# A fused four-layer kernel on one core: grid operations one unit earlier, five copies on another engine, a transposition around a matmul, and a rebuilt opening

## The chip, the core and the metric

One NeuronCore of a Trainium2 chip. Its engines run their own instruction queues in order: TensorE (PE; its weight loads are listed as PEld), VectorE (DVE), ScalarE (ACT), GpSimd (POOL) and SyncE (SP, which here issues most transfers). They wait for each other through semaphores only. The metric is device microseconds of one launch. Everything is float32.

## What is computed

Eight images of 512 x 512 pass through four layers. Cut to what matters:

```python
# L0: one step on a grid; A_grid and B_grid are the same for all eight images
df = -(grad(A0*f, 1) + grad(A1*f, 2)) + 0.5 * (grad2(B0*f, 1) + grad2(B1*f, 2) + 2 * cross(B2*f))
x = maximum(f + df * dt, 0)               # one-sided formulas on the four edges
# L1: attention, 16 heads of 32, and a feed-forward of 2048
x = ln(x) * (1 + scale) + shift           # scale, shift = silu(sin_emb(t)) @ W_ada + b_ada
q, k, v = x @ Wq + bq, x @ Wk + bk, x @ Wv + bv
p = softmax(where(mask, -inf, q @ k.T / sqrt(32) + attention_bias))
x = x + (p @ v) @ Wo + bo
x = x + gelu((ln(x) * g2 + beta2) @ W1 + b1) @ W2 + b2
# L2: one expert of eight per image, the same shape, and a layer norm
# L3: x + strength * response, through a basis of rank 32
```

## The kernel before

The program has three stages, one after the other. `grid_stage` does L0 for image 0 and prepares all that the others need. `attention_stage` does the attention of all eight images, and in the shadow of it L0 for images 1 to 7. `mlp_stage` does both feed-forwards and L3. Rows are spread as (p r): row 4p + r lies on partition p. Nearly every instruction is emitted under `keep_in_program_order`, so the order of the code is the order on each engine; nothing is left to a planner.

**The opening** (`fused_kernel` and `grid_stage`). Loads go out on SP in this order: the coefficient arrays B and A, image 0 (f), `W_ada`, then `load_w` with Wq, Wk, Wv and Wo, then the small rows of `load_rows`. Tiny vectors go out on ACT's queue. Eight hardware semaphores are shared by all SP and ACT transfers in turn, so that a transfer is issued only after the one eight places before it has landed. VectorE builds six coefficient planes (ca, cb, cc, ce, cg, and b2 on ACT) and their products with f (e, g, c, ga, gb, q, t); TensorE adds these up over the rows in four PSUM tiles `l0_r` with an identity or a shifted identity (`add`). The planes are written to DRAM from POOL's queue (`coef_q` and so on) for the later images. The first and last row of all images are computed at once on 64 partitions: `edge_in` loads their inputs, `fe` from the images and `ec` from the coefficients, the latter eight times by a broadcast DMA; the result `xe` is put into image 0 by four small DMAs `x<-xe` and into DRAM (`xed`). TensorE then computes the embedding (`pe`), and image 0 is normed (`stats`, `pow` on POOL, four `tensor_scalar`) and turned by TensorE (`x1_in`).

**A unit of attention.** `units` runs over image b, group of four heads c and row class r, 16 to an image; t = 4c + r numbers them. The loop at the end of `attention_stage` works, for unit i, on `softmax` of unit i, on `turned` of unit i-1, on `values` of unit i-2, and ends with `scores` of unit i+1. Between these it interleaves the jobs of `fill`: blocks of q, k, v and o, each of four matmuls of 512 columns, in two halves. `softmax` is an add and row minimum on VectorE from the scores in PSUM, and an exponential on ACT. `turned` transposes the probabilities on TensorE, four 128 x 128 pieces for each of the four heads into a PSUM tile `tr` of which there are two, and copies each tile to `pt`: the first head of a pair (i == 0) on VectorE, the second on ACT. `scores` writes four PSUM tiles s0 to s3, one buffer each, so a score of the next unit waits until VectorE has read that of this one. `divide`, once in four units, turns the reciprocal sums (`rb`) and scales the context.

**The grid of the next image** is done in these units. `GRID` is a table written by hand: 17 places j, each with operations on half an image: q, e, g, c, a, b are products of a coefficient plane with f, w a difference of two q, capitals and signs are adds into the image, hh the ghost columns, x the step in time, s and n the norm. For image n, places 0 to 7 fall in the units t = 8 to 15 of image n-2, and places 8 to 16 in the units t = 0 to 8 of image n-1. A bar splits a place into a part before and one after `divide`. `grid_early` runs places 0 to 7 of image 1 ahead of the loop. `grid_gate` makes POOL wait for the last grid operation of the unit before, after which it adds the mask to the bias tiles (`add_mask`, two operations of 128 x 1024) of the unit after. `x1_in` transposes the next image's x in unit t = 9, in four pieces, of which two share VectorE and two ACT for the eviction.

Of the kernel before, what the change touches and what calls it, by code (L numbers as in the profile page):

```python
# [11 lines left out]
F32 = mybir.dt.float32  # L12
# [3 lines left out]
AF = mybir.ActivationFunctionType  # L16
# [4 lines left out]
NB = 8  # L21
# [18 lines left out]
def fused_kernel(ctx: ExitStack, tc: tile.TileContext, a: dict):  # L40
# [65 lines left out]
    nc.scalar.dma_start(freq, a["c_freq"])  # L106
    bada = ep.tile([P, 2 * KC], F32, name="bada")
    nc.scalar.dma_start(bada, a["b_ada"])
    nc.scalar.dma_start(sigs, a["safety"][None, :].to_broadcast([P, NB]))
    nc.scalar.dma_start(eidx, a["eidx"][None, :])  # L110
    nc.vector.tensor_scalar(bada[:, 0:KC], bada[:, 0:KC], 1.0, None, ALU.add)
# [27 lines left out]
    nc.scalar.activation(sigs, sigs, AF.Sigmoid)  # L139
# [14 lines left out]

    def embed_out(pe):
        tc.keep_in_program_order(
            nc.vector.tensor_tensor(
                ada, pe, bada[:, :, None].to_broadcast([P, 2 * KC, NB]), ALU.add
            )
        )  # L160
# [4 lines left out]
    def load_w():  # L165
        for n in ("Wq", "Wk", "Wv", "Wo"):
            w[n] = w8(wo8, n)
            nc.sync.dma_start(w[n], a[n].rearrange("(k p) m -> p k m", p=P))
# [5 lines left out]
    def load_rows():  # L174
        nc.sync.dma_start(bqk[:, 0, :], a["bq"])
        nc.sync.dma_start(bqk[:, 1, :], a["bk"])
        nc.sync.dma_start(bvc, a["bv"].rearrange("(k p) -> p k", p=P))
        nc.sync.dma_start(bo, a["bo"][None, :].to_broadcast([P, D]))
# [3 lines left out]
        embed_out,  # L182
# [3 lines left out]
    io = ctx.enter_context(tc.tile_pool(name="io", bufs=1))  # L186
    g2 = const.tile([P, 2, KC], F32, name="g2")
    nc.scalar.dma_start(g2[:, 0, :], a["g2"])
    nc.scalar.dma_start(g2[:, 1, :], a["beta2"])
    b1 = const.tile([P, NJ], F32, name="b1")  # L190
    nc.scalar.dma_start(b1, a["b1"])
# [4 lines left out]
        g2, mhalf,  # L196
# [18 lines left out]
def grid_stage(  # L215
    tc, a, const, small, dram, x, mhalf, ident, load_wada, load_w, load_rows, embed,
    embed_out,
# [27 lines left out]
    with ExitStack() as ctx:  # L245
# [22 lines left out]
        pin(nc.gpsimd.memset(ec, 0.0))  # L268
# [7 lines left out]
        with tc.tile_pool(name="raw", bufs=1) as rp:  # L276
            a0, b0, a1, b1 = (
                rp.tile([P, R, D], F32, name=k) for k in ("a0", "b0", "a1", "b1")
            )

            def edge_in(i, k):
                lo, hi = max(0, W * k - 1), min(D, W * k + W + 1)
                u = slice(lo - W * k + 1, hi - W * k + 1)
                p0 = n * i
                pin(nc.gpsimd.dma_start(fe[p0 : p0 + n, :, u], a["edge_f"][:, :, lo:hi]))
                for side in range(2):
                    p1 = p0 + side * NB
                    pin(
                        nc.gpsimd.dma_start(
                            ec[p1 : p1 + NB, :, u],  # L290
                            a["edge_c"][side : side + 1, :, lo:hi].to_broadcast([NB, 12, hi - lo]),
                        )
                    )

            halves = slice(0, 2), slice(2, 4)
            for h in halves:
                rows_in(b1, a["B"][1], h)
                rows_in(a1, a["A"][1], h)
            rows_in(b0, a["B"][0])
            rows_in(a0, a["A"][0])  # L300
            rows_in(f, a["x"][0])
            rows_in(b2, a["B"][2])
            nc.scalar.dma_start(gw, a["c_ghost"].to_broadcast([P, 16]))
            nc.scalar.dma_start(dth, a["dt"][None, :].to_broadcast([P, NB]))
            load_wada()
            load_w()
            load_rows()
            pin(nc.gpsimd.memset(zi, 0.0))
            pin(nc.gpsimd.tensor_copy(zi[:, 0, 1 : P + 1], ident))
            pin(nc.gpsimd.tensor_scalar_mul(zi[:, 1, 1 : P + 1], ident, -1.0))  # L310
            gate = small.tile([P, 1], F32, name="gate_e", tag="gate_e", bufs=1)
            pin(nc.gpsimd.tensor_tensor(gate, f[:, 0, 0:1], f[:, 0, 0:1], ALU.add))
            for i, k in enumerate(blocks):
                edge_in(i, k)

            for h in halves:
                tt(ca[:, h, :], b1[:, h, :], a1[:, h, :], ALU.add)
                tt(cb[:, h, :], b1[:, h, :], a1[:, h, :], ALU.subtract)
            tt(cc, b0, b1, ALU.add)
            pin(nc.scalar.mul(cc, cc, -2.0))  # L320
            tt(ce, a0, b0, ALU.add)
            tt(cg, b0, a0, ALU.subtract)
            pin(nc.scalar.mul(b2, b2, 0.5))


        wp = ctx.enter_context(tc.tile_pool(name="l0", bufs=1))
# [54 lines left out]
        for m, w, o in (  # L381
            ("q", b2, 1), ("e", ce, 1), ("c", cc, 0), ("g", cg, 1), ("a", ca, 0), ("b", cb, 0)
        ):
            coefs[m] = dram.tile([S + 2 * o, D], F32, name=f"coef_{m}")
            pin(
                nc.gpsimd.dma_start(
                    coefs[m][o : o + S, :].rearrange("(p r) j -> p r j", r=R), w
                )
            )
            if m in "qe":  # L390
                pin(nc.gpsimd.dma_start(coefs[m][0:1, :], w[0:1, 0, :]))
            if m in "qg":
                pin(nc.gpsimd.dma_start(coefs[m][S + 1 : S + 2, :], w[P - 1 : P, R - 1, :]))
# [83 lines left out]
        xed = dram.tile([n, D], F32, name="xed")  # L477
        for i, k in enumerate(blocks):
            pin(nc.gpsimd.dma_start(xed[:, W * k : W * k + W], xe[n * i : n * i + n, :]))
        pe = embed(ps)  # L480
        pin(nc.vector.tensor_scalar(dth, dth, 0.5, None, ALU.mult))
        st = small.tile([P, R, 6], F32, name="ln0_st", tag="ln0_st", bufs=1)
        mv = small.tile([P, R, 2], F32, name="ln0_mv", tag="ln0_mv", bufs=1)
        for r in (0, 3, 1, 2):
            stt(x[:, r, :], acc[r], dth[:, 0:1], f[:, r, :], ALU.mult, ALU.add)
            pin(nc.scalar.activation(x[:, r, :], x[:, r, :], AF.Relu))
        for o, u, c in ((0, 3 * n, 0), (n, n, 2 * W)):
            for side, q_ in ((0, nc.sync), (1, nc.scalar)):
                p, r = side * (P - 1), side * (R - 1)
                e0 = o + side * NB  # L490
                pin(
                    q_.dma_start(
                        x[p : p + 1, r, c : c + 2 * W].rearrange("o (b w) -> o b w", w=W),
                        xe[e0 : e0 + u + 1 : u, :],
                    )
                )
# [24 lines left out]
def attention_stage(  # L521
    tc, a, small, xp, xt, x_home, x1d, grid, ident, sc1, shift, io, wo8, w, rows,
    g2, mhalf,
# [11 lines left out]
    with ExitStack() as ctx:  # L535
        wp = ctx.enter_context(tc.tile_pool(name="aw", bufs=1))
        pp = ctx.enter_context(tc.tile_pool(name="ap", bufs=2))
        ps = ctx.enter_context(tc.tile_pool(name="a_ps", bufs=1, space=PSUM))
# [85 lines left out]
        def k_block(b, c, tag="m"):  # L624
            pr = ps.tile([P, S], F32, name=f"pk_{b}_{c}", tag=tag)
            half = block(
                pr, lambda k: w["Wk"][:, k, c * P : (c + 1) * P], lambda k: x1s[b, k]
            )
            yield half(0)
            yield half(1)  # L630
            t = pp.tile([P, S], F32, name=f"kt_{b}_{c}", tag="kt")
            pin(nc.scalar.activation(t, pr, AF.Identity, bias=bqk[:, 1, c : c + 1]))
            ks[b, c] = t

# [100 lines left out]
        def grid_op(n, op):  # L735
# [62 lines left out]
            0: "q0 q1", 1: "e0 |", 2: "w0 c0 hh", 3: "C0", 4: "+0 -0", 5: "g0 |", 6: "G0 a0",  # L798
            7: "A0 b0 B0", 8: "x0 q2", 9: "e1 | w1 c1", 10: "C1 +1", 11: "-1 g1", 12: "G1 s0",
# [84 lines left out]
        def fill(b, t):  # L884
# [17 lines left out]
            elif t in (1, 5, 9):  # L902
                jobs.append(k_block(b, t // 4 + 1))
            elif t in (2, 3, 6, 7):
                if b:
                    jobs.append(o_block(b - 1, (2, 3, 6, 7).index(t)))
            elif n < NB:
                if t == 11:
                    jobs.append(q_block(n, 0))
                elif t == 13:  # L910
                    jobs.append(k_block(n, 0))
                else:
                    jobs.append(v_block(n, (10, 12, 14, 15).index(t)))
            if n < NB:
                if t == 9:
                    jobs.append(x1_in(n, c) for c in range(KC))
# [67 lines left out]
        def turned(b, c, r, u):  # L984

            bt = bias.pop((b, c, r, u))
            for i in range(2):
# [9 lines left out]
                if i == 0:  # L997
# [49 lines left out]
        load_bias(*units[0])  # L1047
        grid_loads(1, -1)
        mask_in(0, 1)
        load_bias(*units[1])  # L1050
        for c in range(KC):
            x1_in(0, c)
        mask_out(0, 0)
# [3 lines left out]
        grid_early(0)  # L1057
# [5 lines left out]
        mask_in(0, 3)  # L1063
        grid_early(2)
# [44 lines left out]
def mlp_stage(tc, a, small, xp, io, wo8, x1d, ident, eidx, sigs, layernorm, rstd_of, phalf, wl3, g2, b1, first):  # L1109
# [19 lines left out]
    with ExitStack() as ctx:  # L1129
        wp = ctx.enter_context(tc.tile_pool(name="fw", bufs=1))  # L1130
        ap = ctx.enter_context(tc.tile_pool(name="fa", bufs=2))
        ps = ctx.enter_context(tc.tile_pool(name="f_ps", bufs=2, space=PSUM))
# [725 lines left out]
```

## Time and profile before

| | us |
|---|---|
| median of 3 runs | 2807.26 |
| lowest and highest run | 2805.81, 2810.29 |
| the profiled execution, its time | 2809.32 |
| its span, first to last instruction | 2807.5 |

The 1.8 us between the profiled execution's time and its span lie outside the instructions. The stages, from the busy time of each engine in stretches of the span:

| stretch, us | what | PE busy | DVE busy | ACT busy | POOL busy | granted PE clock |
|---|---|---|---|---|---|---|
| 0 to 60 | opening | 33.4 | 43.9 | 11.2 | 24.0 | 0.99 |
| 60 to 107 | norm of image 0, first units | 37.2 | 35.3 | 12.3 | 11.8 | 0.83 |
| 107 to 230 | rest of image 0 | 116.4 | 104.2 | 78.0 | 66.5 | 0.96 |
| 230 to 359 | image 1 | 126.5 | 112.9 | 83.9 | 71.2 | 1.00 |
| 1034 to 1145 | image 7, no grid beside it | 101.7 | 64.1 | 59.4 | 41.2 | 0.97 |
| 1145 to 2050 | feed-forward of L1 and on | 905.0 | 569.0 | 170.0 | 528.1 | 1.00 |
| 2050 to 2807 | experts and L3 | 746.7 | 444.2 | 149.7 | 383.0 | 0.99 |

A line of a timeline in what follows gives start, duration, engine, line of the code, operation, output and inputs, and how many instructions were merged. A bracket at its end is the time that the engine stood idle before it, and what released it. TensorE's durations include waits inside a merged group: four scores take 1.14 us when nothing holds them.

### The profile page before, as it was taken

How to read it: one execution, taken by the hardware profiler on the slowest of the kernel's cores; microseconds unless marked ns; L12 is line 12 of the kernel's file. 1: busy time of each engine (PE TensorE's matmuls, PEld its weight loads, DVE VectorE, ACT ScalarE, POOL GpSimd, SP SyncE). 2: the span in 40 equal slices, each digit the busy share in tenths (PEclk: the TensorE clock that was granted, in tenths of full speed). 3: DMA queues.
4: the chain of work that ended last, by engine and by line, in shares of the span. 5: the costliest groups of instructions: out<-in, count | busy, mean ns of one | idle time of the engine just before them, and what ended most of it. 6: DMA issues, size and time to landing. Idle time of an engine off the chain costs nothing.

```text
span 2807.5 us, 39790 instructions
## 1 busy us (share of the span) xinstructions
PE 2729.1 (97%) x14654; PEld 2011.6 (72%) x14654; DVE 1942.0 (69%) x3581; ACT 1002.8 (36%) x2133; POOL 1503.9 (54%) x1081
## 2 busy tenths in 40 slices
PE   5999999999999998999999999999999999999998
PEld 3455555555555554788888888888888888888886
DVE  6888898988888766576666756655466556556554
ACT  1466666666666666212111211211121121121221
POOL 3455555555555654466566655656456545535633
PEclk9999999999999999999999999999999999999998
DMA  9665657566666554542533444253223133143120
GB/s 300 225 204 180 235 172 241 186 223 214 194 233 191 157 160 158 181 121 49 158 124 83 109 143 124 49 169 120 73 97 125 59 137 128 42 154 113 42 75 31
DMA packets 190400, 405.62 MB, mean 144 GB/s; under 512 B 24104, under 2 KB 28784, under 8 KB 183934
## 3 DMA queue, kind: packets, MB, share of 16 engines
q1 hardware_dynamic: 185192, 391.93, 42.2%
q0 software_dynamic: 3680, 11.07, 3.2%
q8 instruction: 117, 1.92, 0.3%
q14 instruction: 77, 0.63, 0.1%
q10 hardware_dynamic: 1334, 0.07, 0.0%
HBM read 367.32 MB, written 31.50 MB: 142 GB/s over the span
## 4 chain that ended last, share of the span: by engine, by line
PE 86%; DVE 9%; ACT 2%; DMA 2%; issue 1%; SPq 0%; DVEq 0%; ACTq 0%; POOL 0%
PE y L1137 28%; PE u L1137 28%; PE tr L546 6%; PE s L543 4%; PE ctx L543 4%; PE o L543 3%; PE pv L543 3%; PE pq L543 3%; PE pk L543 2%; DVE bt L973 2%; DVE x L663 2%; DVE pt L998 1%; DMA Wo<-in_Wo 1%; ACT bt L978 1%; PE po L1137 1%; PE btr L1140 1%
## 5 line engine op out<-in xcount | busy, mean ns | idle before, releaser
L1137 PE MATMUL y<-wo,act 128*128 128x256 f32 x2560 | 578.9, 381 | 0.0
L950 POOL TENSOR_TENSOR bt<-bt,mk 128x1024 f32<-128x1024 f32 x256 | 543.2, 2142 | 64.2 <-DMA bt<-in_bias 61.2
L1137 PEld LDWEIGHTS y<-wo,act 128*128 128x128 f32 x2560 | 479.4, 190 | 82.2 <-issue 20.6
L978 ACT ACTIVATE bt<-bt,mn 128x512 f32<-128x512 f32 x512 | 365.4, 715 | 115.5 <-DVE mn L973 115.4
L546 PEld LDWEIGHTS tr<-ident,bt 128*128 128x128 f32 x2048 | 228.2, 141 | 167.7 <-issue 115.7
L1137 PE MATMUL u<-bt,wi 128*128 128x256 f32 x1440 | 330.5, 379 | 0.0
L973 DVE CUSTOM_DVE_ANT_0 bt<-s,bt 128x512 f32<-128x512 f32 x512 | 330.4, 682 | 0.0
L1143 DVE TENSOR_TENSOR act<-u,u 128x512 f32<-128x512 f32 x256 | 173.3, 686 | 209.9 <-PE u L1137 132.6
L1137 PEld LDWEIGHTS u<-bt,wi 128*128 128x128 f32 x1440 | 273.5, 190 | 37.2
L546 PE MATMUL tr<-ident,bt 128*128 128x128 f32 x2048 | 279.9, 278 | 18.8 <-DVE pt L998 7.7
L998 DVE COPY pt<-tr 128x512 f32<-128x512 f32 x256 | 175.8, 687 | 113.3 <-PE tr L546 113.0
L1137 PE MATMUL u<-tb,ws 128*128 128x256 f32 x1024 | 242.1, 379 | 0.0
L1137 PE MATMUL y<-t,s 128*128 128x256 f32 x1024 | 234.2, 380 | 0.0
L1000 ACT COPY pt<-tr 128x512 f32<-128x512 f32 x256 | 148.1, 579 | 183.1 <-PE tr L546 180.7
L1137 PEld LDWEIGHTS u<-tb,ws 128*128 128x128 f32 x1024 | 194.4, 190 | 26.5
L1146 POOL TENSOR_TENSOR t<-wo,t 128x512 f32<-128x512 f32 x64 | 104.5, 1647 | 200.5 <-PE y L1137 200.5
L1137 PEld LDWEIGHTS y<-t,s 128*128 128x128 f32 x1024 | 191.1, 190 | 24.1
L1457 ACT ACTIVATE act<-act,b 128x512 f32<-128x512 f32 x128 | 82.9, 711 | 292.4 <-DVE act L1143 292.4
L1457 ACT ACTIVATE act<-act,bi 128x512 f32<-128x512 f32 x128 | 83.8, 713 | 282.6 <-DVE act L1143 282.6
L1143 DVE TENSOR_TENSOR x<-y,x 128x512 f32<-128x512 f32 x96 | 64.5, 685 | 159.0 <-PE y L1137 105.1
L543 PE MATMUL s<-kt,qt 32*128 32x512 f32 x1024 | 171.7, 645 | 2.3 <-DVE mn L973 1.4
L1143 DVE TENSOR_TENSOR u<-u,u 128x512 f32<-128x512 f32 x192 | 131.3, 684 | 58.8 <-PE u L1137 58.8
(314 smaller groups left out, 4283.5 us busy)
## 6 DMA issues: line engine op xcount, KB each, us to landing
bt<-in_bias SPq DMA_DIRECT2D x256, 512.0 KB
wo<-in_W SPq DMA_DIRECT2D x32, 1024.0 KB
wi<-in_Wi SPq DMA_DIRECT2D x32, 1024.0 KB
wo<-in_Wo_e SPq DMA_DIRECT2D x32, 1024.0 KB
wi<-in_W SPq DMA_DIRECT2D x28, 1024.0 KB
gq<-coef_q SPq DMA_DIRECT2D x21, 512.0 KB
x1d<-x SPq DMA_DIRECT2D x8, 1024.0 KB
x<-x1d SPq DMA_DIRECT2D x8, 1024.0 KB
```

Source lines behind the costliest of these rows:

```text
L543: pin(nc.tensor.matmul(out, lhsT=lhsT, rhs=rhs, start=start, stop=stop))
L546: pin(nc.tensor.transpose(out, src, ident))
L663: pin(nc.vector.tensor_tensor(out, x, y, op))
L950: nc.gpsimd.tensor_tensor(bt, bt, mask[b, r][:, None, :].to_broadcast([P, 2, S]), ALU.add)
L973: nc.vector.tensor_tensor_reduce(bt[:, i, :], ss[h], bt[:, i, :], -1.0, 3.0e38, ALU.add, ALU.min, mn)
L978: nc.scalar.activation(bt[:, i, :], bt[:, i, :], AF.Exp, bias=mn, scale=-1.0, accum_out=sums[b, c, r][:, h : h + 1],)
L998: pin(nc.vector.tensor_copy(pt[:, :, r % 2, :], tr))
L1000: pin(nc.scalar.copy(pt[:, :, r % 2, :], tr))
L1137: pin(nc.tensor.matmul(out, lhsT=lhsT, rhs=rhs, start=start, stop=stop))
L1143: pin(nc.vector.tensor_tensor(out, x, y, op))
L1146: pin(nc.gpsimd.tensor_tensor(out, x, y, op))
L1457: nc.scalar.activation(acts[g][:, k, :], acts[g][:, k, :], func, bias=bi[:, j : j + 1])
```

## The change

- `GRID`: w0, C0, +0, g0, G0 and A0 come earlier by one place; q0, q1, e0, c0, hh, -0, a0, b0, B0 and the places from 8 on stay. `grid_early(0)` is called ahead of the first q block.
- `turned`: the first copy of a unit's first pair goes to ACT when the unit turned is t = 1, 3, 5, 7 or 15 of an image, so it is issued in the next unit (t = 2, 4, 6, 8 and 0). That is 40 copies in all.
- `k_block` in unit t = 9 takes `turn`: the first two transpositions of the next x stand between the third and the fourth matmul of k, the other two behind the eviction of k.
- The opening: the coefficients' edge rows are loaded once, on 8 partitions (`ec8`), and spread to 64 by four matmuls with a selection matrix (`sel8`) and four ACT copies. Wv and Wo are loaded behind the first bias tiles, the vectors g2, beta2 and b1 later still. The tiny vectors move from ACT's queue to SP's. The edge rows are put into x as soon as rows 0 and 3 are done, on SP and ACT; the DRAM copy `xed` moves from POOL's queue to ACT's.
- Eight pools get `reuse_waits="tile"`: a tile waits for those that held its memory, no longer for all of the closed pool's.

```diff
+    nc.sync.dma_start(sigs, a["safety"][None, :].to_broadcast([P, NB]))
+    nc.scalar.activation(sigs, sigs, AF.Sigmoid)
...
-    def load_w():
-        for n in ("Wq", "Wk", "Wv", "Wo"):
+    def load_w(*names):
+        for n in names:
...
-    io = ctx.enter_context(tc.tile_pool(name="io", bufs=1))
+    io = ctx.enter_context(tc.tile_pool(name="io", bufs=1, reuse_waits="tile"))
...
+            for i, k in enumerate(blocks):
+                c, u = edge_cols(k)
+                pin(nc.gpsimd.dma_start(ec8[2 * i : 2 * i + 2, :, u], a["edge_c"][:, :, c]))
...
+            for i in range(4):
+                pec = ps.tile([N, 3, W + 2], F32, name=f"pec_{i}", tag="pec", bufs=2)
+                mm(
+                    pec, sel8.rearrange("q s b -> q (s b)"), ec8[:, 3 * i : 3 * i + 3, :],
+                    True, True,
+                )
+                pin(nc.scalar.copy(ec[:, 3 * i : 3 * i + 3, :], pec))
...
         for r in (0, 3, 1, 2):
             stt(x[:, r, :], acc[r], dth[:, 0:1], f[:, r, :], ALU.mult, ALU.add)
             pin(nc.scalar.activation(x[:, r, :], x[:, r, :], AF.Relu))
+            if r == 3:
+                edges()
+        xed = dram.tile([n, D], F32, name="xed")
+        for i, k in enumerate(blocks):
+            pin(nc.scalar.dma_start(xed[:, W * k : W * k + W], xe[n * i : n * i + n, :]))
...
+        def k_block(b, c, tag="m", turn=None):
+            pr = ps.tile([P, S], F32, name=f"pk_{b}_{c}", tag=tag)
+            for k in range(KC):
+                mm(
+                    pr, w["Wk"][:, k, c * P : (c + 1) * P], x1s[b, k], k == 0, k == KC - 1
+                )
+                if k == 1 or k == (2 if turn else 3):
+                    yield
+                if turn and k == 2:
+                    turn(0)
+                    turn(1)
             t = pp.tile([P, S], F32, name=f"kt_{b}_{c}", tag="kt")
             pin(nc.scalar.activation(t, pr, AF.Identity, bias=bqk[:, 1, c : c + 1]))
             ks[b, c] = t
+            if turn:
+                turn(2)
+                turn(3)
...
         GRID = {
-            0: "q0 q1", 1: "e0 |", 2: "w0 c0 hh", 3: "C0", 4: "+0 -0", 5: "g0 |", 6: "G0 a0",
-            7: "A0 b0 B0", 8: "x0 q2", 9: "e1 | w1 c1", 10: "C1 +1", 11: "-1 g1", 12: "G1 s0",
+            0: "q0 q1", 1: "e0 | w0", 2: "c0 hh C0", 3: "+0", 4: "-0 g0", 5: "G0 |", 6: "a0 A0",
+            7: "b0 B0", 8: "x0 q2", 9: "e1 | w1 c1", 10: "C1 +1", 11: "-1 g1", 12: "G1 s0",
...
-                if i == 0:
+                if i == 0 and not (u == 0 and 4 * c + r in (1, 3, 5, 7, 15)):
                     pin(nc.vector.tensor_copy(pt[:, :, r % 2, :], tr))
...
         load_bias(*units[0])
+        load_w("Wv")
         grid_loads(1, -1)
         mask_in(0, 1)
         load_bias(*units[1])
+        load_w("Wo")
         for c in range(KC):
             x1_in(0, c)
+        grid_early(0)
...
         drain(q_block(0, 0))
-        grid_early(0)
         grid_early(1)
...
         mask_in(0, 3)
+        load_late()
         grid_early(2)
```

## The prediction

> **What bounds the kernel now.** I read the page's busy times first, then the chain of work that ended last, then TensorE's timeline image by image. The page says that TensorE sets the pace nearly everywhere, and has one weak slice at the start:
>
> ```profile
> PE 2729.1 (97%) x14654; PEld 2011.6 (72%) x14654; DVE 1942.0 (69%) x3581; ACT 1002.8 (36%) x2133; POOL 1503.9 (54%) x1081
> PE   5999999999999998999999999999999999999998
> ```
>
> The first digit is a slice of 70 us at half: the opening is not TensorE's. The feed-forwards (1145 to 2807 us) are full and untouched, so the change can win only in the opening and in small gaps of attention. The chain in order of time (start, duration, what) says what ends last in the opening, and VectorE's timeline shows what it waits for:
>
> ```profile
> 26.67 34.86 DMA Wo<-in_Wo
> 61.56 3.29 DMA x<-xe
> ...
> 70.00 3.42 PE xtr L546 x16
> ...
> 77.56 4.28 DVE gq L663 x2
> ...
> 90.64 3.05 DVE x L663
> ...
> 106.57 0.60 DVE pt L998
> ```
> ```profile
> 64.76 0.69 DVE L499 BATCH_NORM_STATS2 ln_st<-x 128x6 f32<-128x512 f32 x1 [7.64 <-DMA x<-xe]
> ```
>
> Up to 61.5 us the chain is a transfer: the small edge DMA x<-xe could not be issued before Wo, eight transfers ahead of it, had landed; VectorE stands 7.64 us for it. From 77.56 to about 118 us the chain is VectorE without a break. For attention I took image 2; its neighbours repeat it to 0.02 us, with a period of 128.97 us:
>
> ```profile
> 361.40 1.06 PE L546 MATMUL tr<-ident,bt 128*128 128x128 f32 x8 [0.32 <-DVE pt L998]
> 364.12 1.35 PE L543 MATMUL s<-kt,qt 32*128 32x512 f32 x8
> 378.15 0.66 PE L546 MATMUL tr<-ident,bt 128*128 128x128 f32 x4 [0.80 <-DVE pt L998]
> 380.46 1.85 PE L543 MATMUL s<-kt,qt 32*128 32x512 f32 x8
> 389.44 1.14 PE L543 MATMUL s<-kt,qt 32*128 32x512 f32 x8
> 409.53 1.26 PE L546 MATMUL tr<-ident,bt 128*128 128x128 f32 x8 [0.70 <-ACT pt L1000]
> 412.45 1.85 PE L543 MATMUL s<-kt,qt 32*128 32x512 f32 x8
> 437.67 1.34 PE L546 MATMUL xtr<-ident,x 128*128 128x128 f32 x8 [0.47 <-DVE x L588]
> 439.23 0.66 PE L546 MATMUL rb<-ident,rw 128*128 128x128 f32 x4 [0.22 <-DVE x L588]
> ```
>
> The reader is to see that TensorE stalls only in units t = 0, 2, 4, 6, 8 (VectorE late with a copy or with reading the scores: 1.85 or 1.35 us where a free group takes 1.14) and in t = 9 (xtr). Adding brackets and stretch: t0 0.32+0.21, t2 0.80+0.71, t4 0.21, t6 0.70+0.20+0.71, t8 0.16, t9 0.47+0.28+0.22, together 5.0 us an image. Units 10 to 15 have none.
>
> **Copies to ACT.** 40 copies leave VectorE (0.69 us each, 0.60 from start to start) and cost ACT 0.58. ACT is busy 84 of 129 us. What stands behind the copy on ACT is the second copy, and the third transposition waits for that one (in the program the third waits for ACT, the fourth for the first copy). So each unit needs ACT's slack today: from the end of the second copy to the start of the third transposition it is 1.0 us in t0, t4, t8 (0.9), 0.68 in t2, none in t6, where ACT comes late from two norm operations (1.51 us).
> - t2: VectorE begins the scores at 377.4, not 378.0, and reads the last at 380.5; the third transposition keeps its 376.7 and the fourth no longer waits. The scores end some 0.25 late: 1.51 less 0.25, gain 1.26.
> - t0, t4, t8: stalls of 0.53, 0.21, 0.16 are all under 0.6 and go.
> - t6: the second copy ends at 409.9, not 409.4, so the third transposition starts 0.42 later than today; the stretch of the scores (0.71) and of the transposition (0.20) goes: gain about 0.45.
>
> Sum 2.6 an image, for the six images (1 to 6) that have grid work there: 15.7 us. Image 7 has none of these stalls: 0. Image 0 is paced by VectorE and stalls more (2.37 us before xb in t6, 1.10 and 0.63 behind), but its copy of x from xb holds the same buffers: 1.5 us, between 0 and 6, since its clock also fell (granted 0.60 in 152 to 160 us).
>
> A rule speaks against this. The Trainium skill's "ScalarE: Activation LUTs", Rules for kernel authors, gives such cheap operations to VectorE, up to about three times faster in bf16. At three times 0.69 a copy would hold ACT 2.1 us, overrun every slack above by over 1 us and cost 40 us. The rows for this copy, f32 out of PSUM, say 579 ns on ACT and 687 on VectorE; I take the rows.
>
> **The turn around k.** Between the second and third xtr there will be one k matmul (two passes, 0.86 us). VectorE evicts the first xtr behind its scores at 436.1 to 436.9, and k ends at 437.2: 0.47 and 0.28 go. The third piece's eviction then holds rb by some 0.3 as today by 0.22. k's own eviction comes 1 us later, not needed before t = 11. Gain 0.5, in seven images: 3.5 us; bounds 0 and 0.97.
>
> **The grid moves.** No instruction is added. w0 (1.2 us) comes behind divide in t = 9, so VectorE's first copy of t = 10 is at 441.9, not 441.6; its transposition buffer is needed at 443.6, so it is hidden by the v matmuls (1.72 us); without that cover it would cost 0.9 an image. C0 (1.35) ends t = 10 at 449.1, when the next transposition ends. t = 15 loses A0 (1.2), which helps t0. POOL's gate now follows C0 or w0; the masks it releases (4.2 us) are read a unit (8 us) later. Cost 0.
>
> **The opening.** (a) ACT's first table load starts behind seven DMA issues, one of them waiting, at 7.67; with two issues left it can start at about 2, and Sin, which VectorE's chain awaits, at 9.1, not 10.5: 1.4. (b) SP issues its first six transfers without a wait (today the third waits until 5.81), so VectorE's waits for A and B (1.01, 0.38, 0.23) go: 1.6. (c) So e and all of TensorE's row sums (26.58 to 54.5, no gap) come 3.0 earlier. (d) The edge loads: 0.39 MB in small packets, while DMA moved only 195 to 232 GB/s from 28 to 40 us at a full share against about 400 before and after, i.e. 12 x 190 kB = 2.3 MB or 5.7 us lost. Instead 49 kB at the start, four matmuls and four copies. None is in the trace: nearest, 0.86 us cold a pass for 512 columns and 0.58 a copy; both engines are empty there (PE until 26.58, ACT 6.4 us before cc), so 0, at worst 2.3 if the first loads land after 23. VectorE's wait for ec (1.63) goes too, hidden under the sums. (e) Wv and Wo leave the queue: 2.1 MB at 0.41 MB/us is 5.1 us. With (d), transfers no longer end last. What is late next is TensorE: sums done at 51.4, embedding at 63.4 - 3.0 = 60.4. Rows 0 and 3 are ready at 51.5; x<-xe takes 3.3 (row above), under the coefficient writes perhaps 6; ACT holds the other two relus behind two issues (0.5 each), in the shade of that landing. From landing to xtr today 5.2 us (statistics, pow, norm). So xtr starts between 60.5 and 63; I take 61.3: 8.7 earlier. The four xed issues on ACT (2.0 us on POOL) have 6 us free there.
>
> Here a second rule: "TensorE: Matmul & The Clock Gate", Part 1, halves the clock after an idle window of about 3.4 us. The gap before xtr (6.64) closes, so by the rule xtr and the first q would run at full clock, 1.3 to 2 us more. But the granted clock here was 0.85 in 58 to 60 and 0.50 in 60 to 62, while the embedding's 8-column matmuls still ran; closing the gap does not keep it up. I take 0.
>
> (f) q0 and q1 now precede qt: VectorE stood 3.25 us for pq at 76.89, and fills that, if gq has landed. The loads of f, q and bias can go out at about 55, not 65, as they wait for single tiles; ahead of x<-coef_e stands Wv, ahead of gg Wo, 2.5 us each, against 10 us gained. C0 moves ahead of the first softmax and out of POOL's way: POOL's two mask adds stretched it to 3.12 from 1.35. This ends with the first softmax near 79.3 (90.6 today), v then holds TensorE until 91.5, and the first copy of pt comes at 94.8 instead of 106.5: 11.7 less, bounds 5 and 15.
>
> **The handover.** The first matmul of the feed-forward no longer waits for VectorE's last o (0.88): VectorE's differences follow at once, so I take 0.6. Other pool waits are nothing's last.
>
> **Sum.** 15.7 + 1.5 + 3.5 + 11.7 + 0.6 = 33.0. Against the profiled execution 2809.3 - 33 = 2776; this execution lay 2.1 above the median shown, so 2774.
>
> **Rivals.**
> - *The opening gives little* (0.20): x<-xe waits under 6.3 MB of coefficient writes and q0 waits for gq. For: small DMAs under load took 4.5 to 6.5 us early on (g2 issued at 7.30 held SP until 13.80). Against: those writes should end near 53. Opening 5: 2781.
> - *The gaps of attention stay* (0.11): ACT's second copy is late in every unit, and what VectorE gains is lost. For: t6 already waits for ACT. Against: slack in four of five. Only opening, turn and handover, 15.8: 2791.
> - *Slower* (0.03): the same mechanism past the balance. In each of 40 places the second copy holds the third transposition by a whole copy, 0.58: 23.2 lost, 15.8 gained, 2815. It decides from 0.40 us a place.
> - *The change does not act* (0.02): a wait that remains, such as one for a shared semaphore, keeps x<-xe where it is and the loads with it, and attention wins as little: 2807.
>
> **Numbers.** The forecast (opening and gaps) has 0.64: 2763 to 2784 by its bounds (image 0 to 6, turn to 6.8, opening to 15, copies up to the full stalls; below, opening 8 and t6 nothing). The range that takes in the rivals but the last two is 2763 to 2790. About 0.2%, 5.6 us, is what a measurement can tell from no change: faster 0.95, within 0.02, slower 0.03.
>
> **What will show it.** Right: xtr at 60 to 63; no 7.64 us wait for x<-xe; the first pt near 95; an image in 125.9 us (128.97 now), score groups of 1.14 in t0, t4, t6, t8; in t6 a longer wait for ACT's pt, in t9 none of 0.47. Wrong: transpositions in t0, t2, t4 held by ACT; VectorE idle for gq or x<-coef_e in 60 to 90 us; stalls new in t = 10 to 15.

## The result, and the profile after

The changed kernel took 2777.3 us (median of 4 runs, 2776.19 to 2778.28) against 2808.3 for the kernel before (four runs, 2805.81 to 2810.29): a ratio of 0.9888, with a 95% interval of 0.9875 to 0.9902. The profiled execution took 2778.28 us, its span is 2776.5. The forecast was 2774, range 2763 to 2790.

The first lines of the page (busy time by engine, and TensorE's busy share in 40 slices of 69 us):

```profile
PE 2724.1 (98%) x14662; PEld 2010.2 (72%) x14662; DVE 1931.2 (70%) x3541; ACT 1023.6 (37%) x2177; POOL 1501.0 (54%) x1074
PE   7999999999999998999999999999999999999998
```

VectorE has 40 instructions less, ScalarE 44 more (40 copies and four of the edge rows), and the first slice went from 5 to 7. Where the 31.0 us of the span went, by four marks that both traces have (the first copy of probabilities; the transposition `rb` of t = 9 in image 0 and in image 6; the first matmul of the feed-forward):

| stretch | before | after | gain |
|---|---|---|---|
| start to first copy of probabilities | 106.49 | 95.10 | 11.4 |
| to `rb` in t = 9 of image 0 | 74.80 | 72.06 | 2.7 |
| to the same place of image 6, six periods | 773.81 | 758.19 | 15.6 |
| to the first feed-forward matmul | 188.24 | 186.21 | 2.0 |
| to the end | 1664.2 | 1664.9 | -0.8 |

**The opening.** The chain of waits of the changed kernel (start, duration, what):

```profile
3.96 12.17 DMA a<-in_A
...
36.87 12.14 PE l L251 x28
...
54.37 5.04 DMA xed<-xe
...
62.30 10.09 DMA x<-coef_e
72.41 1.23 DVE x L695
...
95.18 0.61 DVE pt L1029
```

The transfers of Wo and x<-xe are gone from it; ScalarE's issuing of x<-xe (1.81 us) is still in it. Two transfers further on stand in their place: the edge rows to DRAM (5.04 us), and x<-coef_e, 10.09 us from issue to landing. VectorE's timeline shows which waits are left to it:

```profile
53.00 0.69 DVE L523 BATCH_NORM_STATS2 ln_st<-x 128x6 f32<-128x512 f32 x1 [1.49 <-ACT x L515]
54.62 0.67 DVE L523 BATCH_NORM_STATS2 ln_st<-x 128x6 f32<-128x512 f32 x1
72.41 1.23 DVE L695 TENSOR_TENSOR x<-x,gf 128x1024 f32<-128x1024 f32 x1 [3.67 <-DMA x<-coef_e]
```

The statistics come in the order of rows 1, 2, 0 and 3, so the third, at 54.62, is the first that needs the edge rows. It began at 64.76 before, behind the wait of 7.64 us for x<-xe; now it waits for nothing. The 1.49 us ahead of row 1 are new: ScalarE applies its maximum to that row (x L515) only after it has issued two x<-xe. xtr starts at 59.72 (70.00 before), right behind the embedding. Then VectorE stands 3.67 us for x<-coef_e.

**An image.** TensorE's timeline of image 2, the rows that answer to those shown of before:

```profile
347.09 1.14 PE L567 MATMUL s<-kt,qt 32*128 32x512 f32 x8
362.20 2.28 PE L567 MATMUL s<-kt,qt 32*128 32x512 f32 x8
378.01 1.14 PE L567 MATMUL s<-kt,qt 32*128 32x512 f32 x8
391.64 1.06 PE L570 MATMUL tr<-ident,bt 128*128 128x128 f32 x8 [0.74 <-ACT pt L1031]
394.36 1.45 PE L567 MATMUL s<-kt,qt 32*128 32x512 f32 x8
409.45 1.20 PE L567 MATMUL s<-kt,qt 32*128 32x512 f32 x8
418.56 1.40 PE L570 MATMUL xtr<-ident,x 128*128 128x128 f32 x8
```

They are t = 0, t = 2, t = 4, t = 6 twice, t = 8 and t = 9. The waits of t = 0 and 4 are gone (1.14 is a free group), that of 0.47 in t = 9 too. In t = 2 the wait of 0.80 for VectorE's copy is gone, but the scores stretched from 1.85 to 2.28; t = 6 is nearly what it was. From score group to score group the gains are 0.71 in t = 0, 0.60 in t = 2, 0.40 in t = 4, 0.16 in t = 6, 0.10 in t = 8 and 0.69 in t = 9: 2.66, and the period is 126.32 (128.97).

### The profile page after: what moved, and what is told of

It reads as the page before. It is cut to its first block, busy times and chain, and to the rows that moved or that the text cites. A ratio compares the mean times of both kernels' runs of the same rounds, so it can differ in the third digit from the quotient of the medians.

```text
span 2776.5 us, 39855 instructions
## 1 busy us (share of the span) xinstructions
PE 2724.1 (98%) x14662; PEld 2010.2 (72%) x14662; DVE 1931.2 (70%) x3541; ACT 1023.6 (37%) x2177; POOL 1501.0 (54%) x1074
## 4 chain that ended last, share of the span: by engine, by line
PE 92%; DVE 4%; ACT 2%; DMA 1%; issue 1%; SPq 0%; ACTq 0%; DVEq 0%; POOL 0%
PE y L1171 28%; PE u L1171 28%; PE tr L570 8%; PE s L567 5%; PE ctx L567 4%; PE pq L567 4%; PE pv L567 3%; PE o L567 3%; PE pk L567 3%; PE po L1171 1%; PE btr L1174 1%; ACT bt L1009 1%; PE l L251 1%; DVE bt L1004 1%; DVE x L695 1%; PE ytr L1174 1%
## 5 line engine op out<-in xcount | busy, mean ns | idle before, releaser
L1031 ACT COPY pt<-tr 128x512 f32<-128x512 f32 x296 | 167.7, 580 | 166.9 <-PE tr L570 164.0
L1029 DVE COPY pt<-tr 128x512 f32<-128x512 f32 x216 | 148.5, 687 | 98.6 <-PE tr L570 87.3
```

Source lines behind the costliest of these rows:

```text
L1029: pin(nc.vector.tensor_copy(pt[:, :, r % 2, :], tr))
L1031: pin(nc.scalar.copy(pt[:, :, r % 2, :], tr))
```

## The experiments

Times are medians of 4 runs (5 for copies_alone). "Period" is the median of the six from image 0 to image 6, by `rb` of t = 9; within a run they agree to some 0.3 us, mostly to 0.03. "First copy" and "rb 0" are the first and second mark above. Single runs of one kernel lie up to 11 us apart (loads: 2771.95 to 2782.55), so that a median tells little below 4 us; periods and marks tell more.

| kernel | us | ratio to before | period | first copy | rb 0 |
|---|---|---|---|---|---|
| before | 2808.3 | | 128.97 | 106.49 | 181.29 |
| changed | 2777.3 | 0.9888 (0.9875 to 0.9902) | 126.32 | 95.10 | 167.16 |
| no_copies | 2787.55 | 0.9928 (0.9912 to 0.9945) | 127.57 | 95.17 | 171.23 |
| copies_alone | 2797.4 | 0.9962 (0.9948 to 0.9976) | 127.12 | 106.57 | 179.37 |
| no_turn | 2783.89 | 0.9914 (0.9897 to 0.9930) | 127.00 | 95.05 | 167.78 |
| old_grid | 2777.78 | 0.9899 (0.9882 to 0.9915) | 126.44 | 94.60 | 165.05 |
| no_reuse | 2781.31 | 0.9905 (0.9889 to 0.9922) | 126.32 | 96.22 | 166.52 |
| weights_early | 2777.05 | 0.9889 (0.9873 to 0.9906) | 126.33 | 93.99 | 166.04 |
| xed_pool | 2778.12 | 0.9888 (0.9872 to 0.9905) | 126.31 | 92.92 | 166.69 |
| ec_bcast | 2783.16 | 0.9902 (0.9886 to 0.9919) | 126.32 | 96.11 | 170.39 |
| t2_two | 2777.61 | 0.9889 (0.9873 to 0.9906) | 125.71 | 94.89 | 164.74 |
| n0_late | 2781.17 | 0.9898 (0.9881 to 0.9914) | 126.31 | 95.28 | 169.07 |
| loads | 2776.1 | 0.9878 (0.9862 to 0.9895) | 126.32 | 95.39 | 169.28 |
| best | 2771.99 | 0.9873 (0.9857 to 0.9890) | 125.72 | 93.42 | 163.31 |

### The attention stage, part by part

**no_copies** takes the copies out of the changed kernel:

```diff
-                if i == 0 and not (u == 0 and 4 * c + r in (1, 3, 5, 7, 15)):
+                if i == 0:
```

> The changed kernel with the 40 first copies back on VectorE; nothing else differs. Theory (the copies carry the gain of the attention stage): the period of an image goes from 126.32 back to about 128.3, 1.9 to 2.0 us in each of six images, and the time rises by 11 to 13 us, to about 2789. Rival (the moved grid operations and the turn around k carry it): the period stays under 127 and the time rises by less than 4, to at most 2781.

**copies_alone** puts the same condition, and nothing else, into the kernel before:

```diff
-                if i == 0:
+                if i == 0 and not (u == 0 and 4 * c + r in (1, 3, 5, 7, 15)):
```

> The kernel before with the 40 first copies on ScalarE and nothing else. Theory (the copies act by themselves): the period falls from 128.97 to about 127.0, and the time by 11 to 13 us, to about 2796. Rival (they need the moved grid operations, without which VectorE or ScalarE is late elsewhere): the time falls by less than 6, to 2802 or more.

The times bear out the theory in both directions, a little short of its 11 to 13: 10.2 us lost by the one, 10.6 won by the other (against the runs of before made beside it, 2807.98). Of the 9.2 that the profiled run of no_copies lost, 7.5 lie in the six periods and 4.0 in image 0; the end of image 7 gives 2.1 back. The periods say more. Alone, the copies are worth 128.97 - 127.12 = 1.85 an image; taken out of the changed kernel, 127.57 - 126.32 = 1.25. (One of the six periods of copies_alone is 3.7 longer than the others. There, in t = 8 of image 2, VectorE's small operation on grs took 1.99 us, 0.66 to 0.90 in the same place of images 1 and 3 to 6. The scores stretched to 3.41, and the clock was then halved for 3.4 us, so that the contexts took 3.45 us for 1.93.) TensorE's timeline of no_copies in image 2 shows where the 0.6 is:

```profile
366.24 0.66 PE L570 MATMUL tr<-ident,bt 128*128 128x128 f32 x4 [0.80 <-DVE pt L1029]
368.54 1.85 PE L567 MATMUL s<-kt,qt 32*128 32x512 f32 x8
397.61 1.26 PE L570 MATMUL tr<-ident,bt 128*128 128x128 f32 x8 [0.70 <-ACT pt L1031]
```

These are t = 2 and t = 6, as before to 0.01 us. But the wait of 0.32 in t = 0 is not there although VectorE has its copy again. Of the rest of the change only A0, moved from t = 15 to 14, bears on that place; this is read from the order, since no run has the grid moves alone. In t = 0, then, two parts do the same work, and either is nearly enough: 0.71 is gained there without the copies, 0.59 in copies_alone.

**no_turn** puts the transpositions of x behind k again:

```diff
-                turn = (lambda c: x1_in(n, c)) if t == 9 and n < NB else None
-                jobs.append(k_block(b, t // 4 + 1, turn=turn))
+                jobs.append(k_block(b, t // 4 + 1))
...
+                if t == 9:
+                    jobs.append(x1_in(n, c) for c in range(KC))
```

> The changed kernel with the four transpositions of the next x behind the last k block again. Theory (what the two traces say, 0.69 us an image in seven images): the period is 127.0 and the time 4.8 us longer, 2782. The prediction's figure, 0.5 each, would be 3.5 longer, 2781. Rival (the wait was hidden by other stalls of the same unit): no more than 1 us, 2778.

The period is 0.68 longer, and the waits of 0.47 and 0.22 in t = 9 are back. In time it lost 6.6; 2.5 of that lies between image 6 and the feed-forward (188.68 for 186.21), where nothing was changed and where the clock was halved for 10.2 us, not 3.4 (see the end).

**old_grid** restores the table's places 0 to 7:

```diff
-            0: "q0 q1", 1: "e0 | w0", 2: "c0 hh C0", 3: "+0", 4: "-0 g0", 5: "G0 |", 6: "a0 A0",
-            7: "b0 B0", 8: "x0 q2", 9: "e1 | w1 c1", 10: "C1 +1", 11: "-1 g1", 12: "G1 s0",
+            0: "q0 q1", 1: "e0 |", 2: "w0 c0 hh", 3: "C0", 4: "+0 -0", 5: "g0 |", 6: "G0 a0",
+            7: "A0 b0 B0", 8: "x0 q2", 9: "e1 | w1 c1", 10: "C1 +1", 11: "-1 g1", 12: "G1 s0",
```

> The changed kernel with the table of grid operations as it was before; the call for place 0 stays ahead of the first q block. The prediction: no effect, within 2 us, 2776 to 2779. Rival 1 (the moves unload the units t = 0 and 15): the period is 0.3 to 0.6 longer and the time 2 to 4 longer. Rival 2 (they only lengthen t = 9 and 10): faster by 1 to 3.

The prediction's zero nearly holds: the period is 0.12 longer, all of it in t = 0, whose scores take 1.26 us for 1.14, and the time 0.5, within the noise. Copies alone 1.85, turn 0.68 and grid 0.12 add up to 2.65, which is the whole gain of a period.

### Why t = 2 and t = 6 gave so little

**t2_two** takes one more copy from VectorE, in t = 2 only:

```diff
-                if i == 0 and not (u == 0 and 4 * c + r in (1, 3, 5, 7, 15)):
+                if i == 0 and not (4 * c + r in ((1, 3, 5, 7, 15), (1,))[u]):
```

> The changed kernel with the first copy of the second pair on ScalarE too, in unit t = 2 only (units turned with t = 1). Theory (in t = 2 the scores end 1.05 us after VectorE's last read of a score, so that each copy taken from VectorE moves their end by its 0.6 us, no more and no less): the period falls from 126.32 to 125.7, the time by 3.5 to 4, to about 2773. Rival (the two copies in a row on ScalarE come too late for the context matmuls right behind the scores): the period stays within 0.2 or grows.

The period is 0.61 shorter. VectorE's last read of a score and TensorE's scores, in the changed kernel and then in this one (image 2, t = 2):

```profile
362.61 0.68 DVE L1004 CUSTOM_DVE_ANT_0 bt<-s,bt 128x512 f32<-128x512 f32 x1
362.20 2.28 PE L567 MATMUL s<-kt,qt 32*128 32x512 f32 x8
```
```profile
358.98 0.69 DVE L1004 CUSTOM_DVE_ANT_0 bt<-s,bt 128x512 f32<-128x512 f32 x1
359.17 1.68 PE L567 MATMUL s<-kt,qt 32*128 32x512 f32 x8
```

The context matmuls behind the scores start at 364.41 and 360.78, 1.80 us behind the start of that read in both; before the change it was 1.80 as well (380.44 and 382.24). The fourth score is released only when its 0.68 us read ends, and then still has its two passes to run. So a copy moves the end by its own 0.6, whatever waits stood ahead. The time did not follow the period: of the four runs one took 2770.2 and three 2777 to 2778, with a mean granted clock of 0.995 in the first and 0.992 to 0.994 in the others.

**n0_late** moves the norm that keeps ScalarE in t = 6 behind its copies:

```diff
-            13: "a1 | n0 A1 b1", 14: "B1 x1", 15: "s1", 16: "n1",
+            13: "a1 | A1 b1", 14: "n0 B1 x1", 15: "s1", 16: "n1",
```

> The changed kernel with the grid's first norm (n0) moved from place 13 to the head of place 14, so that its two operations of 0.76 us come behind the copies of t = 6 on ScalarE, not ahead of them. Theory (two engines are late in t = 6, and ScalarE only hides VectorE): the wait of 0.74 us for ScalarE's pt goes, the scores behind it stretch to some 2.2 us for VectorE's last read instead, and the period falls by 0.3 at most; in image 0 the wait of 2.37 us before xb shortens by 1.5, and the time falls by 2 to 5, to 2773 to 2775. Rival (ScalarE alone is late): the period falls by 1.2 to 1.5 and the time by 9 to 12, to about 2767.

TensorE in t = 6 of image 0 (two rows) and of image 2:

```profile
135.43 0.75 PE L570 MATMUL xb<-ident,x 128*128 128x128 f32 x4 [0.97 <-ACT pt L1031]
138.68 1.12 PE L570 MATMUL tr<-ident,bt 128*128 128x128 f32 x4 [2.05 <-DVE x L620]
...
395.31 2.32 PE L567 MATMUL s<-kt,qt 32*128 32x512 f32 x8
```

ScalarE's 0.74 is gone from image 2, the scores stretched from 1.45 to 2.32, and the period is the same. VectorE's last read of a score in t = 6 says why, in the changed kernel and then in this one:

```profile
393.94 0.68 DVE L1004 CUSTOM_DVE_ANT_0 bt<-s,bt 128x512 f32<-128x512 f32 x1
```
```profile
395.76 0.69 DVE L1004 CUSTOM_DVE_ANT_0 bt<-s,bt 128x512 f32<-128x512 f32 x1
```

The contexts start at 395.74 and 397.56, 1.80 us behind it in both, and before the change as well (412.43 and 414.23). So VectorE decided t = 6 of this image all along, and ScalarE's wait was covered. In image 0 the 2.37 us before xb became 0.97, and 2.05 appeared behind it, for VectorE. That the time would fall by 2 to 5 was wrong.

### The opening, part by part

**ec_bcast** brings the broadcast back, without `ec8`, `sel8`, the matmuls and the copies:

```diff
-                pec = ps.tile([N, 3, W + 2], F32, name=f"pec_{i}", tag="pec", bufs=2)
-                mm(
-                    pec, sel8.rearrange("q s b -> q (s b)"), ec8[:, 3 * i : 3 * i + 3, :],
-                    True, True,
-                )
-                pin(nc.scalar.copy(ec[:, 3 * i : 3 * i + 3, :], pec))
+                for side in range(2):
+                    p1 = n * i + side * NB
+                    pin(
+                        nc.gpsimd.dma_start(
+                            ec[p1 : p1 + NB, :, u],
+                            a["edge_c"][side : side + 1, :, c].to_broadcast(
+                                [NB, 12, c.stop - c.start]
+                            ),
+                        )
+                    )
```

**weights_early** loads all four weights at the start, and not behind the bias tiles:

```diff
-            load_w("Wq", "Wk")
+            load_w("Wq", "Wk", "Wv", "Wo")
...
-        load_w("Wv")
...
-        load_w("Wo")
```

> The changed kernel with the coefficients' edge rows broadcast to 64 partitions by DMA again, in place of the load to 8 partitions, four matmuls and four copies. The prediction's step (d): the broadcast takes the DMA engines 5.7 us, VectorE waits for it again, xtr comes 3 to 6 us later and the time rises by as much, to 2780 to 2783. Rival (with Wv and Wo gone from the queue it is hidden): under 1 us, 2778.

> The changed kernel with Wv and Wo loaded right behind Wq and Wk, as before. The prediction's step (e): the 2.1 MB take 5.1 us of transfer ahead of the edge rows and of the coefficient writes, xtr comes up to 5 us later, and the time rises by 2 to 5, to 2779 to 2782. Rival (they were only moved to 61 to 70 us, where they stand ahead of x<-coef_e, and the queue had room for them in 20 to 34 us): x<-coef_e lands 2 to 5 us earlier, xtr stays at 59.7, and the time falls by 1 to 4, to 2773 to 2776.

Neither holds xtr back. It starts at 59.64 with the weights early, and with the broadcast at 58.87, even earlier, since the eight-row loads no longer stand beside A and B (VectorE's waits of 0.47 and 0.20 for B and A go). The broadcast costs 1.0 at the first copy: its x<-coef_e lands at 73.4 instead of 72.4. The early weights win 1.1 there: x<-coef_e, with Wv no longer ahead, lands at 69.8; the time stays (2777.05). In the kernel before both loads stood in the queue; in the changed one either may come back without x<-xe being held: Wo lands at 61.5 before, at 38.7 in weights_early, where x<-xe goes out at 49.1. With both back in the changed kernel nothing was run, so it isn't shown which part of the new opening frees x<-xe.

The 5.9 us that ec_bcast lost agree with the expectation by luck. In the profiled run 1.0 is lost at the first copy, 2.2 in image 0 and 2.5 at the end of image 7; in the last two places the clock was halved for longer (see the end). One of its four runs took 2777.21.

**xed_pool** issues the edge rows' DRAM copies on GpSimd's queue:

```diff
-            pin(nc.scalar.dma_start(xed[:, W * k : W * k + W], xe[n * i : n * i + n, :]))
+            pin(nc.gpsimd.dma_start(xed[:, W * k : W * k + W], xe[n * i : n * i + n, :]))
```

> The changed kernel with the four copies of the edge rows to DRAM issued from GpSimd's queue, as before, whose transfers do not share the semaphores of the others. Theory (in the changed kernel SP stood 3 us at 56 to 59 for them, 5.04 us in small packets, and all loads behind went late): the loads of q go out at about 57 instead of 59.7, x<-coef_e lands at about 70 instead of 72.4, and the time falls by 2 to 3, to 2775. Rival (something else holds the loads): no effect, 2777.

SP's queue of the changed kernel, and then of this one (start, time to issue):

```profile
55.80 0.39 SPq L722 DMA_DIRECT2D gf<-in_x  x1
58.83 0.22 SPq L723 DMA_DIRECT2D gf<-in_x  x1
```
```profile
54.60 0.39 SPq L722 DMA_DIRECT2D gf<-in_x  x1
55.03 0.27 SPq L723 DMA_DIRECT2D gf<-in_x  x1
```

The pause of 2.6 us is gone, x<-coef_e lands at 69.6, the first softmax begins 2.8 earlier and the first copy 2.2 earlier: the wait was what it seemed. The time did not fall. By `rb` of image 0 only 0.5 of the 2.2 is left.

**loads** adds another order of the loads to this:

```diff
         load_bias(*units[0])
-        load_w("Wv")
         grid_loads(1, -1)
         mask_in(0, 1)
+        load_w("Wv")
         load_bias(*units[1])
```

> The changed kernel with the edge rows' DRAM copies on GpSimd's queue and with x<-coef_e and gc loaded ahead of Wv and of the second bias tiles. Theory (in 60 to 72 us the order of the loads decides): x<-coef_e lands by 67.5 instead of 72.4, VectorE does not wait for it, the first softmax begins at 73 (77.94), the first copy of probabilities at 91 (95.1). If nothing gives it back, the time falls by 4, to 2773. Rival (image 0 gives it back: the wait of 2.37 us in its t = 6 and the TensorE clock that falls behind it decide when t = 9 is reached): the first copy is at 91 all the same, but rb of image 0 is within 2 us of 167.2 and the time within 2 of 2777.

Both were wrong about the first copy: it stays at 95.39. x<-coef_e lands at 68.9, and the first softmax begins at 76.31, 1.6 earlier. But now v waits 0.97 for Wv and runs 15.67 for 14.00, since the clock is halved from 73.2 to 76.6 behind that wait, and the second q, and with it VectorE, comes late. So this order moves the wait from VectorE to TensorE.

**no_reuse** takes the new argument from all eight pools:

```diff
-    io = ctx.enter_context(tc.tile_pool(name="io", bufs=1, reuse_waits="tile"))
+    io = ctx.enter_context(tc.tile_pool(name="io", bufs=1))
...
```

> The changed kernel with all eight pools waiting for the whole of a closed pool's memory again. Theory (single-tile waits let the loads of the next image out at 53 us and let the feed-forward start at once): the loads of f and q go out some 5 us later, the first copy of probabilities comes 3 to 6 us later, the handover costs 0.9 again, and the time rises by 4 to 7, to 2781 to 2784. Rival (the loads are held by a semaphore shared with the edge rows anyway): under 2 us, 2779 at most.

The loads of f go out at 56.39 instead of 53.45, the first copy is 1.1 later (3 to 6 were expected), the feed-forward waits 0.88 again. But the feed-forward's own span is then 1664.3 for 1664.9, so that the handover is worth 0.2 to 0.3 net. In time 4.0 was lost, with runs from 2778.4 to 2784.5; its profiled run had the changed kernel's span, 2776.6.

### A version that beats both

**best** takes weights_early, xed_pool and n0_late together, gives ScalarE the first copy of either pair in t = 2 and t = 6, and none where image 7 has no grid beside it:

```diff
-                if i == 0 and not (u == 0 and 4 * c + r in (1, 3, 5, 7, 15)):
+                if i == 0 and not (16 * b + 4 * c + r < 104 and 4 * c + r in ((1, 3, 5, 7, 15), (1, 5))[u]):
```

> Five parts together: Wv and Wo loaded behind Wk; the edge rows' DRAM copies on GpSimd's queue; n0 moved behind the copies of t = 6; in t = 2 and t = 6 both first copies on ScalarE; and no first copy on ScalarE where image 7 has no grid work beside it. Theory (each copy taken from VectorE in a unit whose scores it ends is worth its 0.6 us, in t = 6 only once ScalarE is no longer late too): the period falls from 126.32 to 125.1, the first softmax begins at 73 to 75, the time falls by 8 to 12, to 2766 to 2769. Rival (t = 6 stays as it is, and image 0 gives the opening back through the clock): the period is 125.7 and the time 2771 to 2775.

Its four runs (2770.19 to 2775.54) all lie below the changed kernel's four; the medians are 5.3 apart, though the intervals of the two ratios overlap. The rival's figures came true: 125.72 is t2_two's period. In t = 6 the scores take 1.72 instead of 2.32, but a new wait stands in the unit behind, where n0 now is (VectorE's small part of it, gsh, took 1.49 us there, 0.13 in t = 6 of the changed kernel):

```profile
395.68 0.66 PE L570 MATMUL tr<-ident,bt 128*128 128x128 f32 x4 [0.55 <-ACT pt L1031]
```

## Why the prediction was right, and where it was wrong

| term | predicted | shown |
|---|---|---|
| copies, six images | 15.7 | 11.1 alone (6 x 1.85), 7.5 beside the moved grid |
| turn around k, seven images | 3.5 | 4.8 (0.68 each) |
| grid moves | 0 | 0.7 (6 x 0.12) |
| opening to the first copy | 11.7 | 11.4 |
| image 0 behind it, its turn aside | 1.5 | 2.0, of a quantity that varies by 4 |
| handover | 0.6 | 0.2 to 0.3 |
| end of image 7 and the rest (the remainder) | 0 | 0.8, of a quantity that varies by 2.5 |
| sum | 33.0 | 31.0 |

The sum came within 2 us partly by luck: the copies were taken 4.6 too large, the turn, the grid, image 0 and the end together 3.3 too small.

- **The copies** had the right mechanism and too large a size. The failed term is in t = 2: "The scores end some 0.25 late: 1.51 less 0.25, gain 1.26". I let the contexts start some 0.5 us behind the end of VectorE's last read; they start 1.80 us behind its start, 1.12 behind its end, with or without the change, so the gain is the copy's 0.60. For t = 6, "gain about 0.45" was 0.16, and its path was wrong: I took ScalarE's copies to come last there. Their wait grew (0.70 to 0.74), but VectorE's last read decided before and after (n0_late). That read, seen from the start of the unit's scores, came 0.26 earlier, not 0.60: VectorE's divide waits for ScalarE's rbs, which came 0.34 later. t = 0 and 4 gave more than I took (0.71 and 0.40 for 0.53 and 0.21), t = 8 0.06 less. The score groups of 1.14 came in t = 0 and 4, not in t = 6 (1.45) and 8 (1.20), and the period is 126.32, not 125.9.
- **The slower rival** (0.58 in 40 places) and **the gaps stay** are refuted by copies_alone: 10.6 us won.
- **The rule** weighed against the copies foretold a loss of 40 us; the rows, 580 ns on ScalarE and 687 on VectorE after the change, decided rightly. The rule was for bf16; these copies are float32 out of PSUM.
- **The turn**: mechanism right, 0.2 an image too small.
- **The opening**: the sum was right by luck, parts of it not. Steps (a) to (c) hold (TensorE's sums start at 23.12, 3.5 earlier; 3.0 was said), and so does the end of the 7.64 us. xtr came at 59.72, outside "between 60.5 and 63". Steps (d) and (e) did not carry what I put on them: 5.7 and 5.1 us of transfer, of which restoring either costs xtr nothing. VectorE idles 3.67 us for x<-coef_e, a sign that the prediction itself named as wrong. Of "2.5 us each" Wv's part was right (2.6, by weights_early). The term put at nothing was the four xed issues, said to "have 6 us free there": their transfers held SP's queue for 2.6 us and x<-coef_e for 2.8 (xed_pool). C0 did get out of POOL's way, but the operation behind the softmax met the mask adds instead (3.03 us). The first softmax ended at 80.4, 1.1 us later than was said, and v did not hold TensorE until 91.5 but until 87.1; from the softmax to the first copy VectorE worked without a break. The rival "the opening gives little" named the waits of x<-xe and of gq; the first is gone, the second became 0.53.
- **No clock from closing the gap**: right. The clock was 0.50 from 56 to 64 us while TensorE was busy without a break; it rose at 65.6, 5.8 us after xtr began. The first q took 4.79 us for 3.60, hidden by the wait for x<-coef_e.

## What to carry to other kernels

When a wait goes, the gain is not the wait: write down when each engine that the unit needs is done, and take the difference to the next latest, down to the passes that the released instruction still has to run. Two edits that relieve the same place add less than their sum, and undoing one of them in the finished kernel undervalues it; try each alone as well. A small transfer that shares completion semaphores with large loads can hold them all: count what stands between an issue and the one it waits for.

## What the runs showed of the hardware

The same stall does not always cost the same. In t = 6 of image 0 TensorE waits 2.37 us before xb in the changed kernel and in no_reuse alike, 1.1 us later in the second. TensorE in stretches of 2 us (length, busy time and instructions, granted clock, DMA share, GB/s), the changed kernel first:

```profile
134.00:136.00 2.00, 0.19 (x2) 1.00 0.22 27
136.00:138.00 2.00, 1.44 (x8) 0.81 0.65 236
138.00:140.00 2.00, 1.66 (x8) 0.50 0.03 8
```
```profile
136.00:138.00 2.00, 0.32 (x2) 1.00 0.59 176
138.00:140.00 2.00, 1.28 (x12) 1.00 0.26 94
140.00:142.00 2.00, 2.00 (x11) 1.00 0.15 29
```

In the first the clock is halved from 137.2 to 144.1 us, in the second not at all, though its stall is as long; in t2_two it was halved from 135.5 to 138.9. The Trainium skill's "TensorE: Matmul & The Clock Gate", Part 1, calls the window in which activity is counted free-running. The clock records of the 14 traces agree: every halved stretch but the last of a run, which the end of the record cuts, lasts a whole number of times 3.41 us (one to five), and within a run all of them start on one grid of that step, which lies elsewhere in the next run. In the changed kernel the stall (134.19 to 136.56) falls inside one window (133.82 to 137.23). In no_reuse (135.31 to 137.68) the edge at 137.12 divides it, and TensorE idles 1.81 and 1.28 us in the two windows. In the twelve runs in which a window there holds 2.07 to 2.38 us of idle time, the next window is halved. This is not the whole rule: in the kernel before 1.82 us were enough, and xed_pool, ec_bcast, loads and n0_late have a halved window that begins at 149 to 153 us, behind one with only 0.58 to 0.63 us of idle time.

The stretch from the first copy to `rb` of image 0 has the same instructions on TensorE in the changed kernel, no_reuse, weights_early, xed_pool, ec_bcast and loads. It lasts 72.1, 70.3, 72.0, 73.8, 74.3 and 73.9 us, with two halved windows, none, two, three, three and most of a fourth, and three. The end of image 7 takes 186.2 with one halved window and up to 188.8 with three. That is where 1.7 of xed_pool's 2.2 us went. It is also most of why runs of one kernel here differ by up to 11 us: by my estimate a mean clock of 0.995 or 0.992 (t2_two) over 2770 us makes 8. A gain of 2 us ahead of such a stall is decided by where the stall falls.
